# Layer 0's seam, the opening of layer 1's attention and its last unit: three changes of order in a two-layer kernel

## The chip, the cores and the metric

The kernel runs on one core of a Trainium2 chip, as one program. The metric is the time on the device in microseconds (us), lower is better; it is the median of several runs. Engines are named as in the profile: PE is TensorE (matrix products), PEld its loading of weights, DVE is VectorE, ACT is ScalarE, POOL is GpSimd, SP is SyncE, which here only issues DMA transfers.

## The reference

The input has 8 sequences of 512 rows with 256 values each. Two layers follow one another, each with attention and a feed-forward part, all around a residual stream:

```
x = x + L0_attn(layernorm(x))   # 16 heads of 16, causal; its own layernorm again, then w_qkv
x = x + L0_ffn(layernorm(x))    # 704 hidden; inputs, hidden values and weights go through
                                # blockwise FP4 (16 values share a scale: max|x| / 6)
x = x + L1_attn(layernorm(x))   # 16 heads of 16, window of 64 keys, biases, Wq Wk Wv Wo
x = x + L1_ffn(layernorm(x))    # 768 hidden, integer weights times 1/127
# both feed-forward parts: down(silu(gate(x)) * up(x))
```

## The kernel before

The whole residual stream stays in SBUF (tiles x0 to x7, one for a sequence, called a batch here). The four parts of the two layers run one after the other; at each seam the pool of tiles of the old part is released and that of the new one takes its memory, so the first instruction of an engine on a new tile waits for the other engines' last work on the old ones.

*Precision by halves.* Where a product must be more exact than TensorE's fp32r, an operand is split into a high half (a copy to fp32r, on ACT) and a low half (the difference, on POOL or DVE), and three products of halves are summed. `split` does it for the layer 0 feed-forward inputs: ACT makes `fyT0` (L293) and a second, full copy `full` (L294, one buffer), POOL the difference `fyT1` (L295). `project` (L297) sums the pairs of halves in the order high-high, high-low, low-high.

*Order of the work.* A scheduler places the instructions in each engine's queue. Those that are pinned (`pin`, `tc.keep_in_program_order`) keep the order of the program among themselves; each engine, SP's DMA queue too, then works strictly in its queue's order.

*Attention* (`attention`, L360) serves both layers; `banded` is set for layer 1. A unit is half the heads of a batch (8 heads), a quad four heads. For a unit, `load_q` and `load_k` project (PE), and `pieces` makes a bf16 part on ACT and the remainder `qr` or `kr` on DVE. `store` makes the two further bf16 parts (layer 1: the middle one on ACT at L431, the last on POOL at L434), and SP writes the three to HBM. `land` fetches them back, spread over partitions, into one of three buffers `QQ[n]` and `KK[n]`; the third pair is made by `units_tiles` at the beginning of each attention, whose copy of `own` into `kk` runs on DVE (L353). `body` then walks over 32 quads in a software pipeline. At step i it computes the scores of quad i+2 and their maxima (`scores`, `maxima`, DVE), sends the maxima of quad i+1 into `QQ` (`max_rows`), computes the transposed scores of quad i with the Exp on ACT and the masks on POOL (`Outputs.tiles`, L620, L655, L128), and sums quad i-1. Projections, stores and fetches of coming units are hung on certain steps: unit i//2+3 is projected at odd steps, its k is stored and it is fetched at the next even step (r is i % 4, c is i // 4, f1 to f3 are places within a step). `norm` makes the rows `by` of a coming batch on ACT.

*Opening of layer 1's attention.* `opening` runs beside the last tiles of layer 0's feed-forward. `body` then computes the scores of quad 1, sends the maxima of quad 0 (`max_rows(0)`), turns batch 1 (`turned(1, c)`: PE transposes, ACT makes yT, DVE the low half `room`, L192) and projects unit 2.

*Feed-forward of layer 0.* For each of 32 row tiles n, `gated` computes gate and up in two halves (PE, PSUM pairs of which there are three), Silu on ACT (L1233), the product on DVE (L1234). Then the FP4 rounding of the hidden rows `h` runs over four engine steps: multiply by the reciprocal scale on POOL (L229), `mg_h` on ACT (L277), two steps on DVE (L279, L281), multiply by the scale on POOL (L282). Three tiles later `turn_rows` transposes (`ph`, PE; a high half hT0 on ACT, L1250, and a low half on DVE, L1251), and `down` multiplies by `wd_high` and `wd_low`. The inputs of a coming batch pass the same rounding (`fy`) and `split` during the tiles of the batch before. Generators, advanced one step at a time, spread such side work: `late_weights` makes the halves of layer 1's q, k, v weights, `last_weights` loads layer 1's feed-forward weights during its attention.

*Layer 0's seam.* `wd_high` takes the room of qkv_raw (tag "raw") and its ACT copy (L1208) runs while layer 0's attention ends. `wd_low` lies in the new pool, and POOL makes it in one subtract (L1209) after the seam.

## Time and profile before

| what | us |
|---|---|
| median of 3 runs | 1280.49 (1279.89 to 1282.59) |
| profiled execution, its own time | 1288.33 |
| span of the profiled execution | 1286.5 |
| PE busy | 1100.3 |
| DVE busy | 943.5 |
| POOL busy | 698.8 |
| ACT busy | 659.7 |
| layer 0 attention, about 0 to 498.7: PE busy | 416.60 |
| layer 0 feed-forward, to 797.5: PE busy | 252.74 of 298.80 |
| layer 1 attention, to 1127: PE busy | 282.87 of 329.50 |
| layer 1 feed-forward, to the end: PE busy | 148.09 of 159.50 |
| DMA: bytes moved | 99.53 MB, 77 GB/s in the mean |

Times in a profile are counted from the beginning of the span. A line of the timeline has the start, the length, the engine, the line of the kernel, the operation, what it writes and reads, the shapes, and in brackets how long the engine had been idle before it and what ended the idle time ("[3.68 <-DVE room L192]"). A row of the waits has the total in us, the number of times and the longest. The granted clock is a share of TensorE's full clock. A busy share is a mean over a stage, and idle time of an engine costs only where the work that ends last waits for it.

### The profile page before, as it was taken

Reading aid. Unit: us, or ns where it says so; the run is one execution under the profiler, and the core shown is the slowest. Engines: PE = TensorE matmul, PEld = TensorE weight load, DVE = VectorE, ACT = ScalarE, POOL = GpSimd, SP = SyncE. Lnnn points to the kernel's source line nnn. Section 1 sums busy time; section 2 is a strip of 40 time slices with the busy share of each in tenths; the row PEclk is TensorE's granted clock in tenths of the full one; section 3 lists DMA queues with packets and bytes.
Section 4 is the critical chain, followed back from the end, with each engine's and each line's share of the span. In section 5 each row is a group of like instructions: output and inputs, shape, how many; then the busy total and the mean of one; then the engine's idle time right before and its main releaser. Section 6 shows DMA issues by size and latency. Waiting matters only on the chain. (4 is left out here: it accounts for less than half of the span.)

```text
span 1286.5 us, 27214 instructions
## 1 busy us (share of the span) xinstructions
PE 1100.3 (86%) x10910; PEld 819.8 (64%) x10910; DVE 943.5 (73%) x1603; ACT 659.7 (51%) x1008; POOL 698.8 (54%) x821
## 2 busy tenths in 40 slices
PE   4778989788998888788888887788998898889998
PEld 2444444444554445787888777567777776668887
DVE  4699896698788885789799857677776686545553
ACT  3255656465674676444444333455555554455553
POOL 5165564465445566655555533576766675534443
PEclk9899999898998999899999988899999998999999
DMA  8644334443453311000000025476675676000001
GB/s 229 140 96 87 86 74 86 79 94 67 91 116 74 81 18 50 1 1 1 1 1 1 1 72 105 100 165 155 144 149 125 141 164 163 2 1 33 33 26 43
DMA packets 51634, 99.53 MB, mean 77 GB/s; under 512 B 6702, under 2 KB 43568, under 8 KB 44848
## 3 DMA queue, kind: packets, MB, share of 16 engines
q1 hardware_dynamic: 50624, 96.96, 33.9%
q8 instruction: 88, 1.44, 0.5%
q10 hardware_dynamic: 816, 0.79, 0.2%
q14 instruction: 42, 0.34, 0.1%
q0 software_dynamic: 64, 0.00, 0.0%
HBM read 61.02 MB, written 29.36 MB: 70 GB/s over the span
## 5 line engine op out<-in xcount | busy, mean ns | idle before, releaser
L128 POOL TENSOR_SCALAR_AFFINE_SELECT ex<-ex 64x512 f32<-64x512 f32 (+2 forms) x448 | 268.9, 603 | 226.1 <-ACT ex L620 131.3
L620 ACT ACTIVATE ex<-t 128x1024 f32<-128x1024 f32 (+1 forms) x192 | 167.9, 882 | 125.3 <-PE t L609 114.1
L517 DVE TENSOR_REDUCE mx<-s 128x2 f32<-128x1024 f32 (+2 forms) x192 | 196.7, 1036 | 41.1 <-PE s L506 40.3
L1319 POOL TENSOR_TENSOR hT<-gh,hT 128x512 fp32r<-128x512 f32 x48 | 61.6, 1290 | 89.6 <-ACT hT L1318 66.1
L655 ACT ACTIVATE ex<-t 128x1024 f32<-128x1024 f32 x64 | 65.5, 1023 | 86.6 <-PE t L647 81.9
L501 PE MATMUL s<-kk_both,qq_both 96*128 96x512 bf16 (+3 forms) x352 | 84.6, 323 | 20.8 <-DVE mx L517 10.9
L506 PE MATMUL s<-cmask,minus_b 128*128 128x128 bf16 (+2 forms) x352 | 90.4, 257 | 0.0
L540 DVE TENSOR_REDUCE mx<-s 128x8 f32<-128x1024 f32 x64 | 77.6, 1215 | 15.3 <-PE s L535 15.2
L282 POOL TENSOR_TENSOR h<-h,sc_h 128x704 f32<-128x704 f32 x32 | 45.1, 1410 | 79.4 <-DVE h L281 73.6
L674 PE MATMUL po<-ex,vp 128*32 128x512 f32 (+3 forms) x1024 | 83.4, 442 | 1.3 <-DVE kr L418 1.3
L609 PE MATMUL t<-qq_both,kk_both 108*128 108x512 bf16 (+3 forms) x352 | 70.9, 306 | 9.1 <-ACT ex L620 4.7
L1386 DVE SCALAR_TENSOR_TENSOR gh<-ggu,gsl 128x512 f32<-128x512 f32 x48 | 33.2, 691 | 57.1 <-ACT gsl L1384 56.6
L1260 PE MATMUL pd<-wd_high,hT 128*128 128x256 f32 x384 | 61.7, 299 | 11.6 <-DVE hT L1251 7.0
L277 ACT ACTIVATE mg_h<-h 128x704 bf16<-128x704 f32 x32 | 25.2, 788 | 82.7 <-POOL h L229 82.7
L1227 PE MATMUL gu<-wg_wgh,fyT 128*128 128x352 f32 x224 | 65.3, 333 | 2.4 <-DVE h L1234 2.4
L501 PEld LDWEIGHTS <-qq_both 96*128 96x128 bf16 x352 | 33.0, 103 | 51.6 <-issue 38.0
L229 POOL TENSOR_TENSOR h<-h,rc_h 128x704 f32<-128x704 f32 x32 | 46.4, 1449 | 34.1 <-DVE rc_h L228 18.8
L1260 PEld LDWEIGHTS pd<-wd_high,hT 128*128 128x128 f32 x384 | 53.7, 200 | 16.4 <-DVE hT L1251 10.7
L1227 PE MATMUL gu<-wu_wuh,fyT 128*128 128x352 f32 x224 | 62.7, 322 | 0.0
L1375 PE MATMUL ggu<-yT,wg_r 128*128 128x512 f32 x192 | 57.6, 412 | 2.1 <-DVE yT L1319 1.1
L279 DVE SCALAR_TENSOR_TENSOR h<-mg_h,h 128x704 f32<-128x704 bf16 x32 | 40.6, 1269 | 22.4 <-ACT mg_h L277 22.4
L674 PEld LDWEIGHTS po<-ex,vp 128*32 128x32 f32 x1024 | 27.1, 109 | 43.9 <-issue 29.8
(335 smaller groups left out, 3167.9 us busy)
## 6 DMA issues: line engine op xcount, KB each, us to landing
q_hbm<-qp SPq DMA_DIRECT2D x90, 128.0 KB
k_hbm<-kp SPq DMA_DIRECT2D x90, 128.0 KB
qq_both<-q_hbm SPq DMA_DIRECT2D x44, 256.0 KB
kk_both<-k_hbm SPq DMA_DIRECT2D x22, 384.0 KB
qq_both<-q_hbm SPq DMA_DIRECT2D x44, 128.0 KB
kk_both<-k_hbm SPq DMA_DIRECT2D x22, 256.0 KB
qq<-q_hbm SPq DMA_DIRECT2D x20, 256.0 KB
vq<-vp SPq DMA_DIRECT2D x8, 512.0 KB
```

The lines of the kernel that those rows point to most:

```text
L128: nc.gpsimd.affine_select(out=t, in_=t, compare_op=ALU.is_ge, fill=0.0, base=base, pattern=[[0, n] for n in shape[1:-1]] + [[sign, shape[- ...
L501: pin(nc.tensor.matmul(bank[:, a * w : (a + 1) * w], lhsT=q[:KF, hs[j], t * P : w], rhs=k[:KF, hs[j], :w], start=(a == 0), stop=False, ski ...
L506: pin(nc.tensor.matmul(bank.rearrange("p (i k) -> p i k", k=w)[:, :, t * P :], lhsT=minus_b, rhs=cmask[:, : len(part), :], start=False, st ...
L517: nc.vector.tensor_reduce(dst, src, AX.X, ALU.max)
L540: nc.vector.tensor_reduce(mx[:, t2 : t2 + 2, :], sc.rearrange("p t (j k) -> p t j k", k=P), AX.X, ALU.max)
L609: pin(nc.tensor.matmul(bank[:, a * w : (a + 1) * w], lhsT=k[: KF + 12, self.hs[j], t * P : (t + 1) * P], rhs=q[: KF + 12, self.hs[j], t * ...
L620: nc.scalar.activation(ex[:, :banks, :used], sc[:, :banks, :used], AF.Exp, scale=QSCALE)
L655: nc.scalar.activation(ex, sc, AF.Exp, scale=QSCALE)
L674: pin(nc.tensor.matmul(self.o[HP * j : HP * (j + 1), t * P :], lhsT=vp[:, t, 4 * c + j, :], rhs=self.ex[t, j], start=(t == 0), stop=(t == ...
L1227: nc.tensor.matmul(gu[:, i, :352], lhsT=YT[b][l][:, e, t * P : (t + 1) * P], rhs=w[r][:, e, f], start=(n == 0), stop=(n == 3 * NE - 1),)
L1260: nc.tensor.matmul(pd[:, :D], lhsT=hT[l][:, k, :], rhs=wd_halves[r][:, k, :], start=(l == r == k == 0), stop=(l == 1 and k == NH - 1),)
L1319: engine.tensor_tensor(lo, src, hi.bitcast(F32), ALU.subtract)
```

## The change

It has three parts.

1. *POOL's weights at layer 0's seam.* `wd_low` now takes the room of qkv_raw and is made by a generator, `down_low`, in three pieces (an ACT copy of 128x512 and a POOL subtract each) during the last quads of layer 0's attention. `wd_high` moves into the new pool, and its ACT copy stands at the head of ACT's queue behind the seam. POOL's subtracts in `split` and in `late_weights` are pinned. As a result the order of POOL's queue changes: in each batch of layer 0's feed-forward, the two subtracts for fyT stand behind the first multiply of the batch's third tile (h2), where the first of them stood between the second multiplies of the first two tiles (h0 and h1); the three subtracts for the q, k, v weights move from behind fy_1's first multiply to the tiles of batch 1. On ACT, the second copy into `full` moves a few places back, in batches 1, 2, 4 and 5 still ahead of the fourth tile's first Silu.

2. *The order where layer 1's attention begins.* `units_tiles` copies on POOL for layer 1. `max_rows(0)` goes ahead of the scores of quad 1, each half of `turned(1, c)` follows one of its two score blocks, and `maxima(1)` comes after unit 2 is on its way. In `pieces`, the low half of the input is now used last (the pairs are swapped). `norm` of a coming batch is spread over steps r = 1 and r = 2 instead of r = 1 alone; ACT's order of the `by` rows stays as it was, but the middle part of k of each batch's second unit now stands ahead of the next Exp instead of behind it, POOL's last part ahead of the next masks, and on SP the three stores of k go together ahead of the fetches of q.

3. *The last unit a quad sooner.* Unit 15 (batch 7, second half) is projected at step 24 instead of 25, its k is stored at step 25 instead of 26, and it is fetched at step 26 as before. On SP the first load of layer 1's gate weights moves behind this fetch and behind the copies `vq1`.

The matmuls are the same in number and shape.

```diff
--- before.py
+++ after.py
@@ -292,13 +292,18 @@
         full = pool.tile([P, 512], F32, tag="full", name=f"full_{name}", bufs=1)[:, :n]
         nc.scalar.copy(hi, src)
         nc.scalar.copy(full, src)
-        nc.gpsimd.tensor_tensor(lo, full, hi.bitcast(F32), ALU.subtract)
-
-    def project(dst, lhs, rhs):
+        tc.keep_in_program_order(
+            nc.gpsimd.tensor_tensor(lo, full, hi.bitcast(F32), ALU.subtract)
+        )
+
+    def project(dst, lhs, rhs, last=False):
+
 
         n = 0
         pairs = PAIRS if len(lhs) == 2 else ((0, 0),)
         for l, r in pairs:
+            if last:
+                l, r = r, l
             for e in range(NE):
                 pin(nc.tensor.matmul(
                     dst, lhsT=lhs[l][:, e, :], rhs=rhs[r][:, e, :],
@@ -346,18 +351,18 @@
 
         return t.bitcast(BF16).rearrange("p t a (h two) -> p t a h two", two=2)[:, :, :, :, 1]
 
-    def units_tiles(pool, n, what):
+    def units_tiles(pool, n, what, engine=nc.vector):
         q = pool.tile([P, 8, S], BF16, tag=f"qq{n}", name=f"qq{n}_{what}", bufs=1)
         k = pool.tile([P, 8, S], BF16, tag=f"kk{n}", name=f"kk{n}_{what}", bufs=1)
 
-        nc.vector.tensor_copy(
+        engine.tensor_copy(
             k[KF:].bitcast(F32), own[KF:].unsqueeze(2).to_broadcast([32, 8, S // 2])
         )
         return q, k
 
     QK = [units_tiles(qk, n, "both") for n in range(2)]
 
-    def attention(home, banded, stats, norm, spin, wq_s, wk_s, wv_s, qcol, kcol, bv_bc, post, filler):
+    def attention(home, banded, stats, norm, spin, wq_s, wk_s, wv_s, qcol, kcol, bv_bc, post, filler, last_weights):
 
 
 
@@ -402,7 +407,7 @@
 
             pp = psum1(f"p{name}_{b}_{m}")
             ws = halved("qk".index(name), b, w)
-            project(pp, [x[:, :, m * P : (m + 1) * P] for x in ws], xT[b])
+            project(pp, [x[:, :, m * P : (m + 1) * P] for x in ws], xT[b], True)
             if home[2]:
                 t = home[0].tile(
                     [P, 3, S], BF16, tag=f"{name}p", name=f"{name}p_{b}_{m}", bufs=home[2]
@@ -743,7 +748,7 @@
 
         def body():
 
-            q, k = units_tiles(home[0], 2, int(banded))
+            q, k = units_tiles(home[0], 2, int(banded), nc.gpsimd if banded else nc.vector)
             QQ.append(q)
             KK.append(k)
             padded_values(home[0], 1, nc.gpsimd)
@@ -756,22 +761,30 @@
                 fine = fine_halves(home[0])
                 next(fine)
             norm(1)
-            for i in range(1 if banded else 0, 2):
-                for s in scores(i):
+            if banded:
+                max_rows(0)
+                for c, s in enumerate(scores(1)):
                     s()
-                maxima(i)
-            max_rows(0)
-            for c in range(NE):
-                turned(1, c)
+                    turned(1, c)
+            else:
+                for i in range(2):
+                    for s in scores(i):
+                        s()
+                    maxima(i)
+                max_rows(0)
+                for c in range(NE):
+                    turned(1, c)
             load_q(units[2])
             stores(units[2], 0)
             load_k(units[2])
             stores(units[2], 1)
             land(units[2])
+            if banded:
+                maxima(1)
 
 
             last = trail = None
-            ending = filler(home[0]) if banded else None
+            ending = last_weights(home[0])
             for i in range(len(quads) + (2 if banded else 1)):
                 ts, ss, cur = [], [], None
                 if i < len(quads):
@@ -812,10 +825,14 @@
                         at(t, lambda t=t: norm(c + 2, [t]))
                 if banded and r == 3 and c + 1 < B:
                     at(f1, lambda: shifted(c + 1))
-                if r % 2 and i // 2 + 3 < len(units):
-                    at(f1, lambda: load_q(units[i // 2 + 3]))
-                    at(f2, lambda: load_k(units[i // 2 + 3]))
-                    at(f3, lambda: stores(units[i // 2 + 3], 0))
+                up = i // 2 + 3 if r % 2 else len(units)
+                down = i // 2 + 2 if r % 2 == 0 and i else len(units)
+                if banded and i in (NC * B - 8, NC * B - 7):
+                    up = len(units) - 1 if r == 0 else len(units)
+                if up < len(units):
+                    at(f1, lambda: load_q(units[up]))
+                    at(f2, lambda: load_k(units[up]))
+                    at(f3, lambda: stores(units[up], 0))
                 for p, fn in tail.pop(i, ()) if banded else ():
                     at(p, fn)
                 if done is not None and banded:
@@ -824,12 +841,15 @@
                     at(p3, lambda: max_rows(i + 1))
                 if cur and not banded:
                     at(f3, lambda: cur.sums((0, 1)))
-                if r == 1 and c + 2 < B and banded:
-                    for t in range(NT):
-                        at(t // 2, lambda t=t: norm(c + 2, [t]))
-                if r % 2 == 0 and i and i // 2 + 2 < len(units):
-                    at(f1 if banded else p1, lambda: stores(units[i // 2 + 2], 1))
-                    at(f1 if banded else f2, lambda: land(units[i // 2 + 2]))
+                if r in (1, 2) and c + 2 < B and banded:
+                    for t in (0, 1) if r == 1 else (2, 3):
+                        at(2 - r, lambda t=t: norm(c + 2, [t]))
+                if down < len(units):
+                    if not banded or i < NC * B - 6:
+                        at(f1 if banded else p1, lambda: stores(units[down], 1))
+                    at(f1 if banded else f2, lambda: land(units[down]))
+                if banded and i == NC * B - 7:
+                    at(f1, lambda: stores(units[-1], 1))
                 for p in range(max(len(ts), nT if last or done else 0)):
                     if p < len(ss):
                         ss[p]()
@@ -841,12 +861,12 @@
                         fn()
                     if banded and p:
                         next(fine, None)
-                    if banded and i > 4 * B - 6:
+                    if i > 4 * B - 6 and (banded or p == 2):
                         next(ending, None)
                 if ss:
                     maxima(i + 2)
                 last, trail = cur, last
-            for _ in ending or ():
+            for _ in ending:
                 pass
             for n in sorted(tail) if banded else ():
                 for p, fn in tail.pop(n):
@@ -998,6 +1018,17 @@
         def spin0(b, c, dst):
             transposed(dst, Y[b], f"a{b}", [c], (gcol, bcol), True)
 
+        def down_low(pool):
+
+            low = HALVES["wd"] = wp.tile([P, NH, D], F32R, tag="raw", name="wd_low")
+            for k in range(0, NH, 2):
+                high = pool.tile([P, 4, D], F32R, tag="y", name=f"wd_high_{k}", bufs=1)[:, :2]
+                nc.scalar.copy(high, wd1[:, k : k + 2])
+                nc.gpsimd.tensor_tensor(
+                    low[:, k : k + 2], wd1[:, k : k + 2], high.bitcast(F32), ALU.subtract
+                )
+                yield
+
         def post0(b, c, o, rz):
             tmp = ap.tile([P, NT, 4, HD], F32, tag="on", name=f"on_{b}_{c}")
             nc.vector.tensor_tensor(tmp, o, rz, ALU.mult)
@@ -1006,7 +1037,7 @@
 
         opening0, body0 = attention(
             (ap, 1, 2, None), False, stats0, norm0, spin0, qkv_raw[:, :, 0:D], qkv_raw[:, :, D : 2 * D],
-            qkv_raw[:, :, 2 * D : 3 * D], None, None, None, post0, fill,
+            qkv_raw[:, :, 2 * D : 3 * D], None, None, None, post0, fill, down_low,
         )
         for _ in opening0():
             pass
@@ -1152,7 +1183,7 @@
 
     opening1, body1 = attention(
         home1, True, stats1, norm1, spin1, raw1[:, 0], raw1[:, 1], raw1[:, 2], qcol1, kcol1, bv_bc,
-        post1, last_weights,
+        post1, None, last_weights,
     )
     with tc.tile_pool(name="ffn0", bufs=2) as fp:
         both = []
@@ -1174,9 +1205,9 @@
             ]
             for i in range(3):
                 nc.scalar.copy(halves[0][:, i], raw1[:, i])
-                nc.gpsimd.tensor_tensor(
+                pin(nc.gpsimd.tensor_tensor(
                     halves[1][:, i], raw1[:, i], halves[0][:, i].bitcast(F32), ALU.subtract
-                )
+                ))
                 yield
             flat = wp.tile([P, 6 * D], I32, tag="wd1", name="wd2_i")
             nc.sync.dma_start(
@@ -1202,13 +1233,9 @@
 
 
         wd_halves = [
-            wp.tile([P, NH, D], F32R, tag="raw", name="wd_high"),
-            fp.tile([P, NH, D], F32R, tag="wdl", name="wd_low", bufs=1),
+            fp.tile([P, NH, D], F32R, tag="wdh", name="wd_high", bufs=1), HALVES["wd"]
         ]
         nc.scalar.copy(wd_halves[0], wd1)
-        nc.gpsimd.tensor_tensor(
-            wd_halves[1], wd1, wd_halves[0].bitcast(F32), ALU.subtract
-        )
 
 
         rows = [fp.tile([P, NH * P], F32, tag=f"h{i}", name=f"h{i}", bufs=1) for i in range(4)]
```

## The prediction

> **What bounds the kernel now.** I read the engine rows of the page first, then the waits of TensorE, then each seam in the timeline, and last the granted clock by windows.
>
> ```profile
> PE 1100.3 (86%) x10910; PEld 819.8 (64%) x10910; DVE 943.5 (73%) x1603; ACT 659.7 (51%) x1008; POOL 698.8 (54%) x821
> ...
> PE   4778989788998888788888887788998898889998
> ...
> DVE  4699896698788885789799857677776686545553
> ```
>
> TensorE is busy in all stages and issues the same matmuls after the change. So only its idle time (186 us) can be won or lost, and the question is which engine ends each wait. In layer 0's feed-forward loop (slices 17 to 23) VectorE is as full as TensorE. The waits that the change can touch:
>
> ```profile
> PE ph L1246 <- POOL h L282: 14.6, 10, 5.2
> ...
> PE s L535 <- DMA kk_both<-k_hbm: 8.2, 3, 6.0
> ...
> PE pk L303 <- ACT oT L695: 4.9, 1, 4.9
> ...
> PE pq L303 <- DVE room L192: 3.7, 1, 3.7
> ...
> PE s L535 <- DMA q_hbm<-qp: 2.2, 1, 2.2
> ...
> PE s L535 <- DMA kk<-k_hbm: 1.2, 1, 1.2
> ```
>
> They sit at these places of the timeline (start, length, what, in brackets the idle time before it):
>
> ```profile
> 525.48 1.54 PE L1246 MATMUL ph<-ident,h 128*128 128x128 f32 x6 [5.24 <-POOL h L282]
> ...
> 804.71 1.22 PE L303 MATMUL pq<-yT,qkv_wg 128*128 128x512 f32 x2 [3.68 <-DVE room L192]
> ...
> 1083.35 0.42 PE L535 MATMUL s<-kk_both,qq_both 96*64 96x64 bf16 x6 [6.05 <-DMA kk_both<-k_hbm]
> ```
>
> The stretches behind them run slowly (columns: stretch, length, busy time of PE, PEld, DVE, ACT and POOL, granted clock, DMA):
>
> ```profile
> 525.40:529.40 4.00, 3.92 (x15) 3.92 (x16) 3.33 (x4) 1.79 (x3) 3.02 (x4) 0.50 0.02 4
> ...
> 804.70:809.80 5.10, 5.09 (x14) 3.77 (x16) 1.38 (x3) 0.69 (x1) 0.00 (x0) 0.55 0.03 6
> ...
> 1045.00:1051.00 6.00, 6.00 (x91) 4.96 (x91) 4.43 (x7) 3.47 (x6) 5.43 (x9) 1.00 0.70 164
> ...
> 1083.30:1089.30 6.00, 5.95 (x55) 5.65 (x56) 2.18 (x2) 1.60 (x2) 2.27 (x4) 0.51 0.85 252
> ```
>
> **The change part by part.**
>
> *Seam of layer 0.* POOL loses one subtract of 3.51 us at 501.93, which ended at 505.44; instead it makes three of 128x512 near 440 to 447 (1.26 each by L295). There they delay the last k store by some 3.4 us, but its scores run only at 462.8: nothing. ACT's three copies (0.6 each) replace one of 1.48: nothing. But the full copy of `wd_high` (1.48) now stands ahead of fy_1 at 501.89, so fy_1 ends at 505.45 instead of 503.97. VectorE could not use it earlier: its tiny `ve_f` took 2.16 us beside POOL's subtract, and am_x started at 505.38. So this delay costs nothing. POOL's three qkv subtracts (509.66 to 514.4) move into the loop. Then h0's first multiply starts near 512.2 instead of 514.37, fy's second ends near 516.5 instead of 518.63, and with fyT no longer ahead of it h0's second ends near 521.9 instead of 525.43. Gain 3.6. The moved subtracts land between batches 1 and 2, beside VectorE. The Trainium skill ("SBUF — State Buffer", section "SBUF: two separate sides") calls the port pair of the two an exclusive lock, held for the whole instruction, which speaks against this move: 3 x 1.26 = 3.8 us of VectorE time. The rows say that the lock bites where both meet (a 128x704 step takes 1.93 us at 654.18 and 0.88 elsewhere); POOL is idle 5.3 us before one of the three, so I take 1.2. Net gain 2.4; by the rule alone it would be -0.2.
>
> *The loop of layer 0's feed-forward.* Pinning the split in `split` changes the order in every batch, and this is the cost. Before, POOL makes fyT's first half between h0's and h1's second multiply; after, it stands behind h2's first. ACT's second copy into `full` (one buffer) waits for it:
>
> ```profile
> 661.24 0.59 ACT L294 COPY full_f<-pt_f 128x512 f32<-128x512 f32 x1 [2.05 <-POOL fyT L295]
> ...
> 663.40 0.46 ACT L1233 ACTIVATE sl<-gu 128x352 f32<-128x352 f32 x1
> ...
> 666.39 1.13 DVE L279 SCALAR_TENSOR_TENSOR h<-mg_h,h 128x704 f32<-128x704 bf16 x1 [1.16 <-ACT mg_h L277]
> ```
>
> Without fyT in between, VectorE finishes h1 some 0.6 us sooner, so h2's first multiply on POOL runs 663.3 to 664.7 and fyT until 665.95. The copy then runs 666.0 to 666.6. In batches 1, 2, 4 and 5 the Silu of the fourth tile stands behind it on ACT: 666.5 instead of 663.40. Behind that wait the rest of fy, mg_h (667.95 instead of 665.56) and the second Silu. VectorE's next step starts at 668.8 instead of 666.39, its second ends at 670.9 instead of 668.76: 2.1 us late. TensorE, which needs the PSUM buffer that VectorE frees, waits 0.9 + 0.65 us there and then for hT. VectorE's only other pause (1.5 us before mg_x) is at the end of the same chain, so nothing is given back: 2.1 per batch. In batch 3 the copy stands behind the first Silu (0.75), in batch 6 behind mg_h (1.0); batch 0 has room at the seam. Loss 4 x 2.1 + 1.75 = 10.1.
>
> *Opening of layer 1's attention.* VectorE loses the copy into kk (2.51 at 797.97), and `room` needs one score maximum less ahead of it. pq needs yT's second half (PE turns it after the second score, ACT ends near 802.7) and no longer `room`, which is used last. So pq starts near 802.7 instead of 804.71: 2.0. POOL takes the copy, which the trace never shows on POOL: between the memset of 128x2048 (1.8) and four times its 128x512 cast (0.61, 2.4 in all); I take 2.4, for it is a copy. It delays bo_rows and with it ACT's bo_halves to some 804.4 and two_rows to 805.6, just when the first qp can start: covered, but with nothing to spare, and at 4.5 it would cost 2. The slow clock behind the wait (5.1 us at 0.55) should shrink; I take 1.2 of its 2.3. Gain 3.2.
>
> *Every batch of layer 1's attention.* The half of norm that moves leaves ACT's order as it is, but k's store of the second unit now stands ahead of the next Exp. Its kr is there at 946.42 while ACT idles until 948.05, so it is free, and POOL's part ends near 948.85 instead of 953.17. On SP all three k stores then go before the q fetches. The waits for this unit's fetch (2.17 at 886.89, 1.17 at 925.25, 0.71 at 963.38, 1.21 at 1004.80) are all below 4.3: 5.3. In batch 5 kr ends at 1031.24 and the Exp began at 1029.92, so there ACT waits; I take 1.3 for it. The swapped order of projections has `room` ready long before: nothing. Gain 4.0.
>
> *Last unit.* Its k was ready on POOL at 1072.10, the stores landed at 1075.5, the fetch at 1083.3. A quad sooner, POOL ends near 1064.5 (pk now stands behind the values of batch 7). The fetch then lands near 1075.7, before TensorE's 1077.3; the q buffers are free, since their last reader ends near 1062. All of 6.05 goes. The clock behind it: 0.51 over 6.0 us. The Trainium skill ("TensorE: Matmul & The Clock Gate", "What's actually happening") says half rate after an idle window of about 3.4 us, and full again after as long: 1.7 us. By the rows it is 6.0 x 0.49 = 2.9; the same work from pm to pot took 3.63 there and 2.09 at 1047.35, and its scores 0.75 more, so 2.3. The measurement decides: 2.3; by the rule the whole sum would be 0.6 smaller. On the other side quads 24 and 25 now share two PSUM buffers with two more projections: a loss of 1.0. Moving the load of wg behind vq on SP delays only weights that are wanted 45 us later. Gain 7.3.
>
> Sum: -2.4 + 10.1 - 3.2 - 4.0 - 7.3 = -6.8. The profiled execution took 1288.33 (span 1286.5), 7.8 above the median of the runs, 1280.49, and its waits are the same program's, so I take the sum off the median: 1273.7.
>
> **The rivals.**
>
> *The loop pays nothing.* VectorE may gain from having no fyT beside its steps (1.92 and 1.55 us at 658.13 and 660.41 against 0.88), and TensorE's 0.9 may hide elsewhere. Then all gains stand: 1280.5 - 16.9 = 1263.6. Against it: a blocked ACT queue is no matter of contention.
>
> *The loop pays more than all gains (slower).* Its place is ACT's second copy into `full`; its price is the full delay of the Silu, 3.1 us, and some 0.4 for the TensorE waits behind it, in each of six batches: 21. The gains of 16.9 are spent at 2.8 per batch; from there on the change loses. 1280.5 - 16.9 + 21 = 1284.6. For it: VectorE is busy 151 of 172 us in the loop, with no room to catch up.
>
> *The change does not do what it says.* SP works in order: if the last fetch waits for a reader of the old q (quad 25) or queues behind unit 14's traffic, it lands as late as before, and the gain of 7.3 is gone: 1281.0.
>
> **How the numbers follow.** The sum as it stands: 0.45, with its own range 1269 to 1278. The loop free: 0.20. The loop dearer: 0.22. The last unit without gain: 0.13. About 0.2% (2.6 us) is what a measurement of this kernel tells from no change. Faster: nearly all of the first, all of the second: 0.64. Same: most of the fourth and the edges of the first and third: 0.13. Slower: 0.23. With half of each outer case inside, the range is 1262 to 1286.
>
> **What would show it.** Right: no wait over 1 us at TensorE's first score of the last quads; pq near 802 with the clock near 1.0 behind it; ph near 522; a period of layer 0's feed-forward of about 35.4 us instead of 33.3, with ACT waiting some 4 us for fyT ahead of the Silu. Wrong, if that period stays at 33.3 (then 1264), or grows by 3 and more (then slower), or if the fetch of the last unit still ends a wait.

## The result: 0.8% slower, and the profile after

| | median us (range) | runs |
|---|---|---|
| before | 1283.55 (1277.20 to 1290.30) | 18 |
| after | 1294.51 (1287.32 to 1297.85) | 18 |

The ratio is 1.0082, with a 95% interval from 1.0065 to 1.0099: some 10.5 us slower, where 6.8 us faster was forecast. (The prediction took its sum off 1280.49, the median of three runs; the median of 18 is 3.1 above it.) The profiled execution of after took 1289.44 (span 1287.6), among the quickest of its 18, and that of before (1288.33) was 4.8 above its median; so the two profiles lie only 1.1 apart, and a term is read from its stage, not from the two spans.

The engine rows and the slices of the page of after:

```profile
PE 1096.8 (85%) x10910; PEld 813.8 (63%) x10910; DVE 934.7 (73%) x1602; ACT 660.3 (51%) x1011; POOL 693.5 (54%) x824
...
PE   4778989788998898787888878798999898889998
...
DVE  4699896698788884878788876686777676655553
```

TensorE does the same matmuls and is idle 191 us of its span instead of 186: the gains and losses are in its waits again. TensorE's waits of after (total us, times, longest):

```profile
PE ph L1273 <- POOL h L282: 14.4, 11, 3.8
PE gu L1254 <- DVE h L1261: 11.0, 10, 2.7
...
PE po L691 <- issue: 5.5, 4, 3.5
...
PE pk L308 <- ACT oT L700: 4.9, 1, 4.9
...
PE s L540 <- DMA kk<-k_hbm: 3.5, 2, 1.9
...
PE s L540 <- DMA kk_both<-k_hbm: 1.7, 1, 1.7
```

The wait of 3.7 for `room` and the 6.0 within the 8.2 for `kk_both` are gone. Two rows have grown: TensorE's waits for VectorE's product in layer 0's feed-forward (11.0 us), and those at `po` that nothing in the profile ends ("issue", 5.5 us). In before they were:

```profile
PE gu L1227 <- DVE h L1234: 5.4, 4, 3.0
...
PE po L686 <- issue: 3.1, 2, 2.0
```

The timeline of after at the same three places:

```profile
521.94 1.12 PE L1273 MATMUL ph<-ident,h 128*128 128x128 f32 x4 [3.84 <-POOL h L282]
...
808.95 0.79 PE L308 MATMUL pq<-yT,qkv_wg 128*128 128x512 f32 x2 [0.39 <-DVE room L192]
...
1085.56 0.26 PE L691 MATMUL po<-ex,vp 128*32 128x64 f32 x4 [3.55 <-issue]
```

And the windows behind them (the last two figures ahead of the GB/s are the granted clock and the DMA share):

```profile
521.90:525.90 4.00, 3.96 (x15) 3.96 (x16) 2.96 (x5) 1.75 (x3) 2.20 (x2) 0.50 0.02 4
808.90:814.00 5.10, 4.80 (x51) 3.42 (x52) 3.40 (x6) 2.87 (x6) 1.36 (x5) 1.00 0.24 61
1085.50:1091.50 6.00, 5.94 (x111) 5.31 (x110) 1.38 (x2) 2.35 (x4) 1.43 (x4) 0.72 0.99 306
```

`ph` starts at 521.94 (forecast: near 522), and the clock behind `pq` is 1.00 instead of 0.55. So at these two places the change did what was said of it. The ACT queue of after, in the batch of layer 0's feed-forward that the prediction took as its example:

```profile
670.29 0.58 ACT L294 COPY full_f<-pt_f 128x512 f32<-128x512 f32 x1 [4.57 <-POOL fyT L296]
670.77 0.47 ACT L1260 ACTIVATE sl<-gu 128x352 f32<-128x352 f32 x1
```

The second copy into `full` waits 4.57 us for POOL's first subtract, and the Silu stands right behind it. Four copies wait over 3 us for that subtract in after, none in before. The mean period of the loop (third ACT copy to hT of a batch to that of the next, from batch 1 to batch 5) is 35.41 us against 33.48; counted by the first copy it is 35.17 against 33.49. The forecast was 35.4 against 33.3.

### The profile page after: what moved, and what is told of

Its sections match the earlier page's. It is cut to its first block, busy times and chain, and to the rows that moved or that the text cites. A ratio compares the mean times of both kernels' runs of the same rounds, so it can differ in the third digit from the quotient of the medians.

```text
span 1287.6 us, 27220 instructions
## 1 busy us (share of the span) xinstructions
PE 1096.8 (85%) x10910; PEld 813.8 (63%) x10910; DVE 934.7 (73%) x1602; ACT 660.3 (51%) x1011; POOL 693.5 (54%) x824
## 5 line engine op out<-in xcount | busy, mean ns | idle before, releaser
L279 DVE SCALAR_TENSOR_TENSOR h<-mg_h,h 128x704 f32<-128x704 bf16 x32 | 41.0, 1283 | 20.7 <-ACT mg_h L277 20.7
L679 PEld LDWEIGHTS po<-ex,vp 128*32 128x32 f32 x1024 | 27.1, 110 | 43.8 <-issue 29.5
```

Source lines behind the costliest of these rows:

```text
L679: pin(nc.tensor.matmul(self.o[HP * j : HP * (j + 1), t * P :], lhsT=vp[:, t, 4 * c + j, :], rhs=self.ex[t, j], start=(t == 0), stop=(t == ...
```

## The experiments

All ratios are to the kernel before, run beside each on the same chip, with 95% intervals. They are the recorded ones and can differ from the quotient of two medians (b_last_vq: 1282.00 against 1282.01, ratio 0.9977). Three stretches are read from ACT's timeline in every profile, each from one execution: *loop* is the seam and layer 0's feed-forward (last copy of oT in layer 0 to the last copy of hT but two), *opening* runs from there to the first oT of layer 1, and *attention* from there to its 28th oT.

| kernel | median us | ratio | loop | opening | attention |
|---|---|---|---|---|---|
| before | 1281 to 1283 | 1 | 285.4 | 41.5 | 266.7 |
| after_again | 1296.61 | 1.0108 (1.0065 to 1.0151) | 293.2 | 36.2 | 272.3 |
| a_unpin | 1286.61 | 1.0032 (1.0014 to 1.0051) | 285.3 | 37.2 | 269.3 |
| b_pin | 1290.70 | 1.0064 (1.0037 to 1.0091) | 294.1 | 39.8 | 260.9 |
| a_full2 | 1283.45 | 1.0010 (0.9994 to 1.0026) | 284.2 | 36.2 | 269.1 |
| b_seam | 1282.39 | 0.9992 (0.9972 to 1.0012) | 285.4 | 41.5 | 259.5 |
| b_open | 1278.89 | 0.9960 (0.9942 to 0.9978) | 286.0 | 36.4 | 265.6 |
| b_norm | 1289.85 | 1.0056 (1.0031 to 1.0081) | 285.9 | 41.6 | 271.0 |
| b_last | 1282.51 | 0.9997 (0.9981 to 1.0014) | 285.5 | 39.9 | 259.5 |
| b_norm_sp | 1285.08 | 1.0038 (1.0017 to 1.0060) | 286.7 | 40.9 | 260.6 |
| b_norm_pad | 1289.38 | 1.0058 (1.0036 to 1.0079) | 285.2 | 40.9 | 267.8 |
| b_last_late | 1286.31 | 1.0030 (1.0011 to 1.0048) | 285.5 | 41.5 | 264.6 |
| b_last_vq | 1282.00 | 0.9977 (0.9953 to 1.0002) | 285.4 | 41.5 | 266.1 |
| b_last_pad | 1289.50 | 1.0045 (1.0019 to 1.0070) | 285.9 | 41.0 | 265.1 |
| b_pad | 1287.20 | 1.0032 (1.0010 to 1.0054) | 285.9 | 41.8 | 271.1 |
| c_open_last | 1283.89 | 1.0001 (0.9979 to 1.0022) | 285.3 | 37.2 | 268.6 |
| c_all_full2 | 1279.10 | 1.0003 (0.9977 to 1.0029) | 283.3 | 36.2 | 263.0 |
| c_best | 1274.25 | 0.9928 (0.9894 to 0.9961) | 284.2 | 36.2 | 255.8 |
| c_best_pad | 1279.36 | 0.9975 (0.9953 to 0.9996) | 284.5 | 36.2 | 265.3 |

The loop repeats within 1.5 us wherever its code is the same. The attention does not: before, b_pin and b_seam have the same TensorE program there and show 266.7, 260.9 and 259.5. One profile is not enough to size a term of that stage; the ratios are.

### The pin in `split`

Three edits: the pin taken from after (a_unpin), the pin alone put into before (b_pin), and a second staging buffer with the pin kept (a_full2). after_again is after once more.

```diff
 a_unpin:
-        tc.keep_in_program_order(
-            nc.gpsimd.tensor_tensor(lo, full, hi.bitcast(F32), ALU.subtract)
-        )
+        nc.gpsimd.tensor_tensor(lo, full, hi.bitcast(F32), ALU.subtract)
 b_pin: the same lines the other way round, in the kernel before
 a_full2:
-        full = pool.tile([P, 512], F32, tag="full", name=f"full_{name}", bufs=1)[:, :n]
+        full = pool.tile([P, 512], F32, tag="full" if name.endswith("0") else "full_1", name=f"full_{name}", bufs=1)[:, :n]
```

> The changed kernel as it is, for a second profile and for the runs that the others are compared with. Theory: about 10 us above the kernel before (ratio 1.008), of which the loop of layer 0's feed-forward is the whole loss (its period 35.4 us against 33.3, about +11.5 us from the seam to the end of the loop), and the parts behind it gain some 3 to 7 us in this profile as in the first (opening about -4, last unit about -3.5, steady attention of layer 1 between -4 and +4). Rival: the loss of a typical run lies in layer 1's attention, in waits for fetches and in waits with no releaser, and the second profile shows an offset of +10 us or more there.

> The changed kernel with the pin in split taken away alone; VectorE's and POOL's halves in the loop of layer 0's feed-forward stand again in the order of before. Theory (ACT's second copy into full is blocked by the pinned order and holds back the Silu): the loop's period falls from 35.4 to about 33.3 us, 10 to 12 us less than the changed kernel, so the whole is 0 to 3 us below the kernel before (ratio 0.998 to 1.0). Rival one (the seam and the moved qkv subtracts cost the loop, not the order of the split): the period stays above 34.5 and the whole within 3 us of the changed kernel. Rival two (the loss is in layer 1): the loop falls but the whole stays 5 us or more above the kernel before.

> The kernel before with the pin in split added alone. Theory: its loop of layer 0's feed-forward takes the period of the changed kernel, 35.4 us, and the whole is 9 to 12 us above the kernel before (ratio 1.007 to 1.0095): the pin alone is as large as the whole result, and the other edits together are worth about nothing. Rival (the pin costs only together with the moved qkv subtracts): less than 4 us.

> The changed kernel with a second buffer for full in split (the two halves take turns), the pin kept: POOL's order stays that of the changed kernel but for one batch, and ACT's second copy no longer waits for POOL's first subtract. Theory (the blocked copy on ACT is the cost): the Silu of the fourth tile starts some 3 us sooner in its batch, the period falls to 33.3 to 33.8 us, 8 to 11 us less than the changed kernel. Rival (POOL's order itself, with fyT later and VectorE beside other POOL steps, is the cost): the period stays at 35 or above, less than 2 us gained.

Without the pin the loop is back at 285.3 and the whole 10 us below after; the pin alone costs the kernel before 0.64%, 8.2 us. a_full2 keeps POOL's order of after but for one batch, and still its loop takes 284.2. Its ACT queue at the same copy:

```profile
656.92 0.59 ACT L294 COPY full_f<-pt_f 128x512 f32<-128x512 f32 x1
...
660.03 0.47 ACT L1260 ACTIVATE sl<-gu 128x352 f32<-128x352 f32 x1
```

The copy has no idle time before it. So it is the blocked ACT queue, and not POOL's order, that costs some 8 to 9 us: the theory holds, its rival falls. But a_unpin is still 4.1 us above before, where 0 to 3 below was expected. Something else lost what the opening gained (37.2 against 41.5), and its attention of 269.3 against 266.7, one profile each, points to layer 1's attention: for this rest rival two of a_unpin is nearer.

### Each other part alone

Four kernels, each the kernel before with one part of the diff: the weights' moves without the pin in `split` (b_seam), the opening with the swapped products (b_open), the moved half of `norm` (b_norm), the last unit (b_last). b_norm's whole edit is

```diff
-                if r == 1 and c + 2 < B and banded:
-                    for t in range(NT):
-                        at(t // 2, lambda t=t: norm(c + 2, [t]))
+                if r in (1, 2) and c + 2 < B and banded:
+                    for t in (0, 1) if r == 1 else (2, 3):
+                        at(2 - r, lambda t=t: norm(c + 2, [t]))
```

> The kernel before with the weights' moves at layer 0's seam alone (wd_low made in the last batch of layer 0's attention, the qkv subtracts pinned behind it in the loop), without the pin in split. Theory: ph starts 3.6 us sooner, as forecast, but the three subtracts (1.26 us each on POOL) then stand among the loop's steps of batches 1 and 2 and give 2 to 3.5 us back, so the end of the loop is 0 to 2 us sooner; ratio 0.9985 to 1.0. Rival (the forecast): 2.4 us faster at the loop's end, ratio 0.998. Rival two: the loop is 2 us or more slower, ratio 1.001 and more.

> The kernel before with the new order at the opening of layer 1's attention alone (VectorE's copy on POOL, the turn of yT between the scores, the swapped order of the projection's products). Theory: 3 to 5 us gained at the first oT of layer 1, and the swapped order of the products costs nothing behind it: ratio 0.996 to 0.998. Rival (the swapped order makes pq and pk wait or hold PSUM longer in the steady batches): the gain is gone by the end of layer 1's attention, ratio 0.999 to 1.003.

> The kernel before with the half of norm moved from the batch's second quad to its third in layer 1's attention alone, which puts the second unit's k store ahead of the next Exp on ACT and its three stores ahead of the q fetch on SP. Forecast: 4 us gained, ratio 0.997. Theory now: the Exp that stands behind the store's piece, and the q fetch that stands behind three k stores, cost as much or more; the waits move to other quads and layer 1's attention takes 0 to 5 us more, ratio 1.0 to 1.004.

> The kernel before with the last unit projected and stored a quad sooner alone. Forecast: the 6.05 us wait for the last fetch goes, 7.3 us gained, ratio 0.994. Theory from the changed kernel's profile: half is given back in the quads 24 to 26, which share PSUM and DMA queues with two more projections, so 3 to 4 us gained, ratio 0.997. Rival: the fetch collides with the values' traffic and nothing is gained, ratio 0.999 to 1.002.

The five parts alone, b_pin among them, multiply to 1.0064 x 0.9992 x 0.9960 x 1.0056 x 0.9997 = 1.0069, inside the interval of the result. Their own intervals together leave 0.5% either way, so this is a rough agreement; but two terms of the forecast are missing. The moved half of `norm` costs 7 us instead of gaining 4, and the last unit gains nothing instead of 7.3. b_seam's moves are worth nothing at the end of its loop: counted from the last oT of layer 0, its first hT comes 1.9 us sooner than in before, in batch 2, behind the moved subtracts, 1.1 later, and at the end of the loop at the same time.

### Why the moved half of norm costs

b_norm leaves TensorE's and VectorE's order as in before. TensorE's timeline in one batch, first of b_norm, then of b_seam (which has the order of before there and runs 0.34 us ahead):

```profile
1001.92 0.30 PE L535 MATMUL s<-kk,qq 96*64 96x64 bf16 x6 [1.69 <-DMA kk<-k_hbm]
...
1005.35 0.42 PE L647 MATMUL t<-qq_both,kk_both 108*64 108x128 bf16 x4 [2.42 <-issue]
```

```profile
1000.14 0.36 PE L535 MATMUL s<-kk,qq 96*64 96x64 bf16 x7 [0.26 <-DMA kk<-k_hbm]
...
1001.75 0.25 PE L647 MATMUL t<-qq_both,kk_both 108*64 108x64 bf16 x2 [0.55 <-issue]
```

SP's queue ahead of it, in the same two kernels:

```profile
985.90 2.25 SPq L437 DMA_DIRECT2D k_hbm<-kp  x3
988.27 1.77 SPq L447 DMA_DIRECT2D qq<-q_hbm  x4
991.11 2.58 SPq L447 DMA_DIRECT2D kk<-k_hbm  x3
993.74 0.52 SPq L398 DMA_DIRECT2D vq<-vp  x1
```

```profile
987.58 3.41 SPq L437 DMA_DIRECT2D k_hbm<-kp  x2
991.04 0.92 SPq L447 DMA_DIRECT2D qq<-q_hbm  x2
993.37 1.23 SPq L447 DMA_DIRECT2D kk<-k_hbm  x3
994.70 0.52 SPq L398 DMA_DIRECT2D vq<-vp  x1
```

The stores and the fetch of `kk` begin sooner, as forecast: its issue begins 2.6 us sooner against TensorE. It lands 1.4 us later. From 989.8 on the DMA engines of b_norm are full (shares of 0.95 to 1.18 in each window of 1.5 us to 1001.8), in b_seam from 992.5 on (0.93 to 1.03), and both have moved nearly the same bytes by 1001.8 (3.73 and 3.70 MB since 976). Behind the wait for `kk` comes a second one, in the middle of a row of Exp products, with no releaser. The two stop TensorE for 4.1 us of 5.1, and the clock falls. The windows from the 17th to the 21st oT of layer 1, b_norm and b_seam:

```profile
981.56:1025.32 43.76, 37.32 (x684) 30.47 (x684) 29.37 (x57) 21.86 (x33) 26.52 (x38) 0.92 0.64 131
```

```profile
981.23:1019.72 38.49, 35.33 (x684) 28.54 (x684) 30.17 (x57) 21.86 (x34) 26.50 (x38) 1.00 0.68 149
```

The same 684 matmuls take 5.3 us more: 3.3 more idle time and 2.0 at the slower clock. But one pair is thin evidence. In before's own profile, with SP's order of b_seam, the same stretch takes

```profile
982.89:1025.86 42.97, 39.44 (x690) 32.24 (x689) 29.43 (x57) 21.95 (x33) 26.53 (x38) 0.92 0.61 134
```

with a wait of 1.21 for `kk`. The other traces say more: the five kernels with the moved half and SP's new order, and no matmuls put in front (b_norm, after, after_again, a_unpin, a_full2), take 42.7 to 43.8 us here, each with both waits; of the ten without the moved half six take 37.9 to 39.3 us and four, before among them, between 40 and 45. From the 5th to the 9th oT b_norm takes 4.4 more than b_seam, but the old order itself ranges from 37.0 to 44.2 there (b_open). Two kernels test it: SP's order of before pinned by hand while ACT and POOL keep b_norm's (b_norm_sp), and b_norm with other code positions (b_norm_pad, below).

```diff
 b_norm_sp, the order on SP in these five units:
-   k, k, k, q, q, q, q, kk, kk, kk
+   k, q, q, k, k, q, q, kk, kk, kk
```

> The kernel before with the moved half of norm, as in b_norm (kr's piece ahead of the Exp on ACT, the subtract earlier on POOL), but with SP's order of before in these five units: one k store, two q fetches, two k stores, two q fetches. b_norm alone cost 7 us. Theory (SP's three k stores in a row, ahead of the q fetch, bunch the transfers: kk's fetch and TensorE's next 16 KB of instructions land later): most of the 7 us is gone, ratio 0.998 to 1.002. Rival (the piece ahead of the Exp on ACT and the masks behind the subtract on POOL are the cost): ratio stays at 1.004 to 1.007.

In b_norm_sp every wait of 1 us or more for a fetch is gone but the last unit's (5.43), as the prediction had it for the earlier piece on ACT, and the attention takes 260.6 in its profile. A wait of 3.39 at 1000.63 with no releaser remains, at the same Exp products. The ratio, 1.0038, lies between both theories and its interval overlaps b_norm's; so in this profile the fetch waits disappear with SP's old order. But b_norm_pad, with the new one, has only one of over 1 us ahead of the last unit's (1.08), and how the 7 us divide between the bunched order and the rest is not settled.

### The wait that no semaphore ends

In b_last the wait for the last fetch is gone, yet TensorE stops a little earlier, between two matmuls of one sum:

```profile
1066.89 0.28 PE L686 MATMUL po<-ex,vp 128*32 128x64 f32 x4
1072.03 0.32 PE L686 MATMUL po<-ex,vp 128*32 128x64 f32 x2 [4.86 <-issue]
```

These are quad 26's sums, in which before has no such stop. The page's row of DMA queues (packets, MB), the same in both kernels, gives a candidate:

```profile
q8 instruction: 88, 1.44, 0.5%
```

Those are 16.4 KB each; for TensorE's 21,820 matmuls and weight loads that would be 248 to a packet. The DMA rows of windows of 0.25 us find one q8 packet starting in the window from 1069.0 in b_last, 3.0 us ahead of TensorE's going on; in b_norm it is 1002.25 and 1005.35, in after 1082.25 and 1085.56. Where b_seam waits only 0.55, the packet came at 998.5, 3.25 ahead. So TensorE seems to go on some 3 us after its packet starts, and stops when the packet starts late.

Counting settles what stops there. Number TensorE's recorded instructions (matmuls, weight loads and the sequencer's) from the beginning. In layer 1's attention the 20 traces of this case have 77 stops of over 0.8 us with no releaser, and 73 of them come at a number that leaves 193 to 196 when divided by 256. The other four stand at the first score on a unit just fetched, where a late fetch is the likely cause. So these stops lie at the edges of groups of 256 instructions. In b_last SP issued the fetch of `kk` (768 KB), `vq` (896 KB) and four weight loads (1.5 MB) from 1059.8 to 1067.0, ahead of that packet. Three kernels take this apart (excerpts of their edits below), and b_pad does to before what b_last_pad does to b_last:

```diff
 b_last_late (b_last, weight loads held back to quad 29):
+                pin(nc.gpsimd.memset(flat[:, 0:1], 0))
                 nc.sync.dma_start(flat, w[c * P : (c + 1) * P, :])
 b_last_vq (b_last, the last shifted(7) moved to quad 28, weights behind it):
+                pin(nc.gpsimd.memset(VQ[b % 2][:, 1, 0, 0:1], 0.0))
 b_last_pad, b_pad (in front of everything):
+    pad = psum1("pad")
+    for _ in range(64):
+        pin(nc.tensor.matmul(pad[:, :1], lhsT=minus_b, rhs=minus_b[:, :1], start=True, stop=True))
```

> The kernel before with the last unit's part alone, as in b_last, but the four loads of layer 1's feed-forward weights (wg_i, wu_i, 384 KB each) held back from quad 27 to quad 29 by a one-column memset on POOL ahead of each. Theory: in b_last TensorE stood 4.86 us in quad 26's sums for its next instructions, whose 16 KB packet came at 1069.0, behind kk's fetch, vq's two loads and the four weight loads that SP issued from 1059.8 to 1067.0; without the four it comes some 3 to 4 us sooner and 3 to 5 us are gained over b_last, ratio to the kernel before 0.996 to 0.998. Rival (kk's fetch and vq alone fill the queues, or the stall is no matter of transfers): the wait in quad 26 or 27 stays above 3 us, ratio 0.999 to 1.001. Second rival: later weights make layer 1's feed-forward start later, ratio above 1.001.

> b_last with the last batch's vq loads (512 and 384 KB) held by a one-column memset on POOL until quad 28's masks, and the weight loads behind them on SP. Theory (instructions queue behind data on the DMA engines; kk's fetch and vq are 1.6 MB, some 9 us at 190 GB/s, and the packet came when they were through): the packet comes after kk's fetch alone, about 4 us sooner, the stall in quad 26's sums falls from 4.9 to 1 us or less, and 3 to 5 us are gained over b_last: ratio to the kernel before 0.996 to 0.998. Rival one (the stall is no matter of the data ahead of it): it stays above 4 us. Rival two (vq then lands too late for quad 28's sums): a wait for vq takes its place, ratio 0.999 to 1.002.

> b_last with 64 matmuls of 128x128 by 128x1 put in front while TensorE waits for the first load, so that every later TensorE instruction stands 128 places (half of a 16 KB packet of 256) further on; no other work is changed. Theory (packets of instructions): the stall leaves its place in quad 26's sums by 64 matmuls, into that quad's scores or Exp products, and has another length, 0 to 5 us; the time moves by some us either way. Rival (a semaphore or a PSUM buffer that the profile does not show): the stall stays at the same two sums with 4.5 to 5.2 us.

> The kernel before with the same 64 matmuls in front. Theory: the waits with no releaser in layer 1's attention (1.84 at 854.13, 1.03 at 865.45, 2.03 at 982.36 in the first profile) change place and length, and the time moves by up to 4 us, either way, by the place of the code alone. Rival: ratio 0.999 to 1.001 and the same waits at the same instructions.

Holding the weights back changed nothing at the stop (5.09, the packet at 1077.0, when `kk` and `vq` were nearly through), and from the 28th oT to the last hT of layer 1 b_last_late takes 185.8 us against b_last's 184.4: that theory fell. Holding `vq` halved the stop, and putting 64 matmuls in front took it out of quad 26's sums altogether. The stop of b_last_vq, in the same sums, and that of b_last_pad, in quad 27's transposed scores:

```profile
1084.29 0.32 PE L688 MATMUL po<-ex,vp 128*32 128x64 f32 x2 [2.42 <-issue]
```

```profile
1077.87 0.33 PE L651 MATMUL t<-qq_both,kk_both 108*64 108x128 bf16 x6 [3.71 <-issue]
```

No work and no semaphore changed between b_last and b_last_pad but the place of the code, so the stop belongs to the instruction stream. Its length goes with the data ahead of the packet: 3.5 to 5.2 us in the eight kernels with the last unit's part, no matmuls in front and `vq` right behind `kk`, 2.42 in both with `vq` held (b_last_vq, c_best). Counted along TensorE's timeline, the new place lies exactly 64 matmuls ahead of the old one. b_last_vq's gain over b_last, 0.2%, is within the two intervals. b_pad is the reminder: the kernel before, with nothing but 64 tiny matmuls in front, is 0.32% slower. Its stops fall elsewhere (1.98 at 939.59, 1.61 at 1044.62, 2.44 at 1061.14); that they make up all of the 4 us is not shown.

> b_norm with the 64 matmuls of b_pad in front. b_norm was 1.0056 and b_pad 1.0032 of the kernel before. Theory (the moved half costs by where packets of instructions meet the bunched transfers): with the edges half a packet on the cost over b_pad is another, between -3 and +4 us, ratio to the kernel before 1.001 to 1.006. Rival (it costs by itself, through the later fetches): again 7 us over b_pad, ratio 1.0075 to 1.010.

Over b_pad the moved half of `norm` costs 1.0058 / 1.0032, 0.26% or 3.3 us, with intervals of 0.2% on either side: no gain here either, and not told apart from the 7 us at the old code position. The profiles suggest that the code position has a part in it: from the 17th to the 21st oT all four kernels with matmuls in front take 37.8 to 38.7 us, b_norm_pad too, and none has the pair of waits. How large this part is stays open.

### What the parts make together

> The kernel before with the opening's part (which gained 4.0 us alone) and b_last_late, without the pin in split, without the moves at layer 0's seam and without the moved half of norm. Theory: the parts add up, 4 us plus what b_last_late gains, 6 to 9 us below the kernel before, ratio 0.993 to 0.996. Rival (the swapped order of the projection's products moves the transfers, and a wait comes back): ratio 0.996 to 0.999.

> The changed kernel with the second buffer for full (pin and seam kept), the four weight loads held back to quad 29, and the moved half of norm taken back. Theory: a_full2 was level with the kernel before while it held the moved half of norm (7 us alone); without it and with b_last_late's gain it is 8 to 11 us below the kernel before, ratio 0.9915 to 0.994. Rival (the moved half of norm costs only in the old surroundings): ratio 0.996 to 1.0.

> The version that the parts point to: pin in split with a second buffer for full, the moves at layer 0's seam, the opening's part, the last unit's part with vq held as in b_last_vq; the half of norm stays where it was. Theory: 4 us of the opening, 1 to 3 of the second buffer, 3 to 5 of the last unit: 7 to 11 us below the kernel before, ratio 0.9915 to 0.9945. Rival (the parts behind the opening meet other packets and queues, and do not add up): ratio 0.996 to 0.999.

> c_best with the 64 matmuls of b_pad in front. c_best was 0.9928 of the kernel before. Theory (the loop's, the opening's and half of the last unit's gains are not of code position, the rest of layer 1's attention is): 2 to 5 us of it are lost, ratio 0.995 to 0.9985. Rival (all its gain is code position): ratio 1.0 and above.

c_open_last and c_all_full2 hold the weights back with the four memsets; from the 28th oT to the last hT of layer 1 they take 186.5 and 188.1 us against 183.3 in before, one profile each. Both are level with before, above what their theories said. c_best has the seam and the pin with the second buffer, the opening, and the last unit with `vq` held, and leaves `norm` where it was: 0.9928 (0.9894 to 0.9961), about 9 us below the kernel before and 20 below after. With 64 matmuls in front it is at 0.9975; against b_pad, which carries the same, that is again 0.57% less. So its gain over a kernel with the same offset stays about 7 us, while the offset moves both by some 4 to 6.

## Why the prediction was wrong, and where it was right

*Seam of layer 0: the place right, the net not shown.* `ph` came at 521.94. But of the 3.8 us that after gains there b_seam gains only 1.9, so half of it needs the pinned split. By batch 2, behind the moved subtracts, b_seam goes from 1.9 us ahead of before to 1.1 behind it: 3.0 us, where the prediction took 1.2 for them. At the end of the loop the two are level. Forecast -2.4, measured -1.0 (-3.6 to +1.5), which excludes neither the forecast nor nothing.

*Loop: right.* Forecast +10.1 by ACT's second copy into `full`; b_pin +8.2 (4.7 to 11.7), its loop stretch +8.7; in after the period is 35.41. a_full2 shows the mechanism.

*Opening: right, a little small.* Forecast -3.2; the stretch is 5 us shorter, b_open as a whole -5.1 (-7.4 to -2.8). The slow clock went altogether (1.00 in after), where 1.2 of its 2.3 us was taken. No price of POOL's copy showed.

*Every batch of layer 1's attention: wrong, the step that failed first.* The prediction took all four fetch waits (5.3) as gone because SP's k stores "go before the q fetches". ACT's and POOL's part of the step was right: in b_norm_sp, with SP's old order, the fetch waits do go. SP's new order, booked as part of the gain, was none: in b_norm two of the four waits are still there (1.94 at 882.47, 1.69 at 1001.92), the second for a fetch that was issued 2.6 us sooner than b_seam's and landed 1.4 later, through full DMA engines; at a third place TensorE stops 1.89 us for its instructions instead (924.02). Stops of over 0.8 us with no releaser come to 8.3 us in b_norm's attention, against 4.9 in before and 2.8 in b_seam; the prediction has no term for them. The 5.3 us was also the sum of a single profile: at the fourth of these places before waits 1.21 and b_seam, with the same order, 0.26. Forecast -4.0, measured +7.2 (4.0 to 10.4): 11 us of the miss. The loss itself is shown; its division between late fetches and late instructions is not.

*Last unit: the wait went, the gain did not.* "All of 6.05 goes" held. The step did not ask what would be late next: TensorE's own instructions, which stop it for 4.86 us in b_last and 3.55 in after. The clock, for which the step booked 2.3 us, is at 0.72 over the 6 us behind the new stop. Forecast -7.3, measured -0.4 (-2.4 to +1.8): 7 us. The forecast's rival of no gain here had the right size for the wrong reason, for the fetch did not queue on SP: in b_last its issue began at 1059.8, in b_seam at 1069.3, 6.6 us sooner against TensorE (b_last is 2.9 ahead there).

*The rival that ended slower* put the loss into the loop, 21 us or 3.5 a batch, with all gains spent at 2.8; the loop lost 1.7 to 1.9 a batch, about as the forecast itself had it. So that rival had the sign by luck: the sign came from the two terms above. Both moved transfers sooner into stretches where the DMA engines are then full, and neither priced what is then late, data or instructions.

## What to carry to other kernels

When stores and fetches are moved sooner in a stage where the DMA engines are already full, cost the landing, not the issue, and ask which transfers now stand in one row and what else comes through them. A pinned order needs a look at the staging buffers along it: here one more buffer for `full` took back what the pin cost. And before a difference of 0.3% is explained, run the old kernel with a few idle instructions in front: that alone was worth as much here.

## What was not expected of the hardware

TensorE's own instructions arrive in packets of 16.4 KB; nearly all its stops without a releaser (73 of 77) lie 256 instructions, or a multiple of it, apart, and where data filled the DMA engines ahead of a packet it stood 2 to 5 us between two matmuls of one row. The Trainium skill ("Runtime: NRT & Kernel Launch", section "Instruction fetch mechanics") says that each engine streams its instructions in 16 KiB blocks through a queue of its own, at a cost that is "mostly hidden". The packet's size agrees; where the DMA share had been near 1.0 the cost was not hidden (4.86 us in b_last, 3.55 in after, 2.42 in b_norm).
